# First batch without the limits of later batches, vectors loaded as rows, and an order planned on other durations

## The chip, the cores and the metric

The kernel runs on one core of a Trainium2 chip. The metric is the device time of one execution in microseconds (us); the time of a kernel is the median of its runs. The engines are PE (TensorE matmul, with its weight loads shown as PEld), DVE (VectorE), ACT (ScalarE), POOL (GpSimd) and SP (SyncE, which here only issues DMAs; ACT issues DMAs too).

## What is computed

Sixteen graphs (the batch) of 1024 nodes with 256 features each pass through two layers, all in float32, with a 0/1 adjacency matrix of 1024x1024 per graph. Cut to what matters:

```
# layer 0: attention with 8 heads of 32, masked by adjacency
q, k, v = heads(x @ Wq), heads(x @ Wk), heads(x @ Wv)
e    = leaky(q @ k.T)                      # leaky: max(e, 0.2 e)
attn = softmax(where(adj > 0, e, -9e15), axis=-1)
h    = layernorm(attn @ v) * g1 + b1
x    = layernorm(concat(h, x) @ Wffn.T) * g2 + b2 + x
# layer 1: two graph attentions, then a feed-forward
for W, a in ((W1, a1), (W2, a2)):
    Wh = h @ W
    e  = leaky(Wh @ a[:256] + (Wh @ a[256:]).T)
    h  = softmax(where(adj > 0, e, -9e15), axis=1) @ Wh
h = layernorm(x + h) * g_ln1 + b_ln1
out = layernorm(h + relu(h @ w_ff1 + b_ff1) @ w_ff2 + b_ff2) * g_ln2 + b_ln2
```

The kernel leaves out the shift by the maximum in the softmaxes and counts, per batch, that all sums and scores stay in a safe range. A second, general path follows behind a test of that count; it does not run on these inputs.

## The kernel before, in words

**Work of one batch.** `project` loads x in four pairs of row tiles (`x_pair`, L430, DMA issued by ACT) and transposes them on PE. `mask_part` (L382) loads one tile of 128 rows of the adjacency, as int32 halves of 128x512 (DMA issued by ACT), turns it to 0/-1 in fp8 on DVE (L400), transposes it on PE (L409) and copies it to the mask (ACT, L413). Batch 0 does this in 16 parts of one half each, the other batches in 8 parts of two halves. `qk_part` (L446) projects a group of four heads to q or k for 512 nodes (PE, L460), splits the result in a high and a low half (ACT L463, DVE L465) and stores both to DRAM (SP, L469). `load_stacks` (L521) loads the halves of one head back as stacked operands (SP, L543).

For each of the 8 heads and each of the 8 tiles of 128 keys, one tile of 128x1024 scores goes through a fixed chain: PE multiplies (L576) into a PSUM buffer of which there are two; ACT, or in batch 0 ACT or DVE, scales by 0.2 (L594, L592); DVE takes the maximum with the PSUM tile (L596), which frees the PSUM buffer; ACT takes the exponential (L599); POOL multiplies by the mask (L603); PE sums the weighted values (L625). There are five SBUF buffers `p` for tiles between L594 and L625. That is 64 tiles per batch. `all_scores` takes both PSUM buffers before it issues two tiles of scores; `all_values` consumes two tiles at a time.

The rest of the batch (`rest`, L966: layer norms, the graph attentions L812 to L820, L849 and L874, the feed-forward L914 to L942) runs beside the scores of the following batches.

**What sets the order.** The instruction order of each engine is written out by the program itself. Each piece of work is a generator that yields a cost per engine (`on(PE=..., DVE=...)`), takes and gives buffers of pools, waits for events, and has an aim, a due time. The class `Order` always issues, of the pieces that could start within a window of 300 ns, the one with the earliest aim. The costs and the aims (`AIM`, as shares of `SLOT`, 253 us) decide the order alone: they add no wait. A piece that gets its operands late still waits on the chip, and so does all that stands behind it on its engine. `pace(b)` is the aimed spacing of score pairs: `SLOT/32`, shortened by `fast0`, `fast1` and `fast15` for batches 0, 1 and 15.

**Limits that the planner keeps.** `adj` (2) limits adjacency parts under way, `stage` (2) limits parts of q and k under way, `pair` (18) is the pool of 128x512 float32 buffers for most small tiles. `prepare` (L1010) loads the vectors and weights of the later stages once, beside batch 0; eight vectors are loaded as columns, one number per partition (`load_cols`, L286).

Of the kernel before, what the change touches and what calls it, by code (L numbers as in the profile page):

```python
# [9 lines left out]
FT = mybir.dt.float32  # L10
# [24 lines left out]
class Order:  # L35
# [98 lines left out]
    def run(self):  # L134
        while self.active:
# [33 lines left out]
            if delay:  # L169
                self.transfers = max(self.transfers, end + 1000) + 1450 * max(1, round(cost / 500))  # L170
                th["ready"] = max(end + delay, self.transfers + 1200)
                th["last"] = None, 0
# [52 lines left out]
def unshifted_path(  # L225
# [23 lines left out]
    NSCORE = 4 * NT  # L249
    SLOT = 253e3  # L250
    PACE = SLOT / (H * NT // 2)


    AIM = dict(x=0.818, x_step=0, mask=0.747, mask_step=0.0264, qk0=0.614, qk1=0.898, qk_step=0.0231, v0=0.832,
               v1=0.974, v_step=0.0591, rows=-0.244, rows_step=0.0408, first0=0.12, first1=0.252,
               graph0=-0.009, graph1=0.21, graph_step=0, second=0.355, second_step=0.0335, normed=0.78,
               normed_step=0.026, ff_wait=(None, 0, 1, 0), ff=(0.532, -0.011, 0.487, 0.497), ff_step=0.0386,
               fast0=0.521, fast1=0.85, fast15=0.832, lead=3.15)

# [25 lines left out]

    def load_cols(v, name):  # L286
        t = const.tile([P, v.shape[0] // P], FT, name=name)
        nc.sync.dma_start(t, v.rearrange("(c p) -> p c", p=P), allow_slow_non_contiguous=True)
        return t

    def load_row(v, name):
# [8 lines left out]
    w12 = const.tile([P, DC, YW + 2], FT, name="w12")  # L300
    right = const.tile([P, B, 4], FT, name="right")
    k = {}

# [10 lines left out]
    def evacuate_by(n):  # L314

        return on(DVE=190 + 1.06 * n, ACT=250 + 0.87 * n)

# [65 lines left out]
    def mask_part(b, t, halves):  # L383

        n = len(halves)
        ints = []
        yield take("adj")
        for kh in halves:
# [9 lines left out]
        for i, ai in enumerate(ints):  # L398
# [3 lines left out]
            yield give("pair")  # L402
        yield give("adj")
        yield take("misc")
# [14 lines left out]
    def make_mask(b, t0):  # L419
        yield take("mask")  # L420
        masks[b] = buf([P, NT * N], "mask", "mask", F8)
        parts = [(t, (kh,)) for kh in range(NH) for t in range(NT)] if b == 0 else [(t, (0, 1)) for t in range(NT)]
        for n, (t, halves) in enumerate(parts):
            yield start(mask_part(b, t, halves), t0 + (AIM["mask"] + AIM["mask_step"] * n) * SLOT)

# [20 lines left out]
    def qk_part(b, g, o, nh):  # L446
# [3 lines left out]
        for u in range(nh * 2, nh * 2 + 2):  # L450
            yield wait(("xT", b, u))
        yield take("stage")
        yield take("pair")
# [3 lines left out]
        high, low = (buf([P, HALF], "pair", n) for n in ("high", "low"))  # L457
        yield on(PE=1720)
        for dc in range(DC):
# [11 lines left out]
        yield give("pair")  # L471
        yield give("stage")
        yield fire(("qk", b, g, o, nh))
# [37 lines left out]
    def project(b, t0):  # L511
        yield take("xT")
        xTs[b] = buf([P, DC, N], "xT", "xT")
        for u in range(NP):
            yield start(x_pair(b, u), t0 + (AIM["x"] + AIM["x_step"] * u) * SLOT)
        yield start(make_mask(b, t0), t0 + 0.5 * SLOT)
        for g in range(H // G):
            yield start(project_qk(b, g, t0 + AIM[("qk0", "qk1")[g]] * SLOT), t0)
            yield start(project_v(b, g, t0 + AIM[("v0", "v1")[g]] * SLOT), t0 + (0.8, 1.0)[g] * SLOT)

# [35 lines left out]
    def all_scores():  # L556
        for b in range(B):
            yield wait(("stack", b, 0))
            t0 = begin[b] = work.now
            if b + 1 < B:  # L560
                yield start(project(b + 1, t0), t0)
            for h in range(H):
                yield wait(("stack", b, h))
                q, kk = stacks[b, h]
                for d in range(NT // 2):
                    due = t0 + (h * NT // 2 + d) * pace(b)
                    yield aim(due, AIM["lead"] * PACE)
                    yield take("scores")
                    yield take("scores")
                    ps = [psum.tile([P, N], FT, tag="scores", name="ps_s") for _ in range(2)]  # L570
                    yield on(PE=900)
                    for i in range(2):
                        t = 2 * d + i
                        for nh in range(NH):
                            cols = slice(nh * HALF, (nh + 1) * HALF)
                            nc.tensor.matmul(ps[i][:, cols], kk[:, t * P:(t + 1) * P], q[:, cols],  # L576
                                             start=True, stop=True)
                    if d == NT // 2 - 1:
                        yield give("stacks")
                    for i in range(2):  # L580
                        yield start(weights(b, h, 2 * d + i, ps[i]), due + i * PACE / 2)

# [117 lines left out]
    def rows_pair(b, u):  # L700
# [23 lines left out]
        for i, t in enumerate(tiles):  # L724
            yield on(PE=1720)
            for dc in range(DC):
# [76 lines left out]
    def attend(b, s, big, rows, j, second, sums):  # L803
# [5 lines left out]
        for nh in range(NH):  # L809
            yield wait(("first", b, s, nh))  # L810
        yield on(DVE=1270, shared=True)
        nc.vector.scalar_tensor_tensor(e, first[:, 0, :], second[:, j:j + 1], first[:, 1, :],  # L812
                                       op0=OP.mult, op1=OP.max)
        yield on(DVE=1250, shared=True)
        nc.vector.scalar_tensor_tensor(e, mask_of(b, j), -1.0, e, op0=OP.mult, op1=OP.mult,  # L815
# [29 lines left out]
    def products(pa, cols, big, rows, i, width):  # L845
        for half in range(2):
            yield on(PE=6.68 * width)
            for j in range(half * NT // 2, (half + 1) * NT // 2):
# [14 lines left out]
    def normed_pair(b, u, big, y2):  # L863
# [6 lines left out]
        for i, t in enumerate(tiles):  # L870
            for half in range(2):
                yield on(PE=1720)
                for j in range(half * NT // 2, (half + 1) * NT // 2):
                    nc.tensor.matmul(pa[:, i * D:(i + 1) * D], big[:, j, t * P:(t + 1) * P], y2[:, j, :D],  # L874
                                     start=(j == 0), stop=False)
            yield on(PE=430)
            as_rows(pa, i, x1, i)
# [27 lines left out]
    def hidden(hid, rT, hp, done):  # L905
# [3 lines left out]
        part = hid[hp] = buf([P, 2, 2 * P], "pair", "hid")  # L909
        yield on(PE=1720)  # L910
        for i in range(2):
# [16 lines left out]
    def feed_forward(b, u, rT):  # L928
# [9 lines left out]
        for i in range(2):  # L938
            for half in range(2):
                yield on(PE=1720)  # L940
                for hc in range(half * HC // 2, (half + 1) * HC // 2):
                    nc.tensor.matmul(pa[:, i * D:(i + 1) * D], hid[hc // 2][:, hc % 2, i * P:(i + 1) * P], wf2[:, hc, :],  # L942
                                     start=(hc == 0), stop=False)
            yield on(PE=430)
            as_rows(pa, i, rT, i)
# [64 lines left out]
    def prepare():  # L1010
# [6 lines left out]

        for name, v in (("g1c", g1), ("b1c", b1), ("g2c", g2), ("b2c", b2), ("gl1c", g_ln1), ("bl1c", b_ln1),
                        ("bf1", b_ff1), ("bf2c", b_ff2)):
            yield load(1, 6000)  # L1020
            k[name] = load_cols(v, name)
        for name, v in (("gl2", g_ln2), ("bl2", b_ln2)):
# [26 lines left out]
        def product(wT, dc, by, width):  # L1049
# [4 lines left out]
            return emit  # L1054

        for ic in range(2 * DC):
            yield from piece(300, D, wffnT[:, ic, :], flips(wf, ic))
# [350 lines left out]
```

## Time and profile before

| What | us |
|---|---|
| median of 3 runs | 4526.02 (4524.72 to 4531.43) |
| the profiled execution's own time | 4521.66 |
| its span, first to last instruction | 4519.9 |
| PE busy in the span | 4333.5 |
| DVE busy | 3305.8 |
| ACT busy | 2893.4 |
| POOL busy | 2454.4 |
| first score matmul (L576) of batches 0, 1, 2, 3 starts at | 45.1, 253.8, 510.3, 790.8 |
| of batches 4, 5, ..., 15 at | 1061.4, 1332.1, ..., 4037.8 |
| last matmul of values (L625) of batch 15 starts at | 4297.4 |

How to read it: the span is 1.8 us shorter than the time of the same execution, and the median of the runs is 4.4 us above that execution. The starts of the batches cut the span in stages. From batch 3 on they stand 270.6 us apart, each time. The records of PE in the trace show a float32 matmul as two records and a transpose or a matmul of the stacked scores as one.

### The profile page before, as it was taken

The page shows a single profiled execution, that of the slowest core. Times are in us where ns is not written, and L with a number is a line of the kernel's source. Part 1 is how long each engine was busy: PE and PEld are TensorE (multiplying, and loading weights), DVE is VectorE, ACT ScalarE, POOL GpSimd, SP SyncE. Part 2 cuts the span into 40 slices and gives each one's busy share as a digit, 9 for nine tenths or more (in the row PEclk, how much of TensorE's full clock was granted, in tenths as well). Part 3 has the DMA queues.
Part 4 walks back from the last instruction along what each step waited for, and adds up shares of the span by engine and source line. Part 5 has one row for each costly group of instructions (what it writes and reads, how often), then busy time and mean ns, then how long its engine had stood idle before and what let it go on. Part 6 is the DMA issues. An engine that isn't in the chain of part 4 may idle for free.

```text
span 4519.9 us, 57125 instructions
## 1 busy us (share of the span) xinstructions
PE 4333.5 (96%) x20298; PEld 2875.2 (64%) x20298; DVE 3305.8 (73%) x5246; ACT 2893.4 (64%) x4030; POOL 2454.4 (54%) x1544
## 2 busy tenths in 40 slices
PE   6778999999999999999999999999999999999999
PEld 3345656667666676666667666676666767666587
DVE  4776778777787777768777787777768777776854
ACT  4556666676666666666666666666676676666631
POOL 3655665565565545655565565545655565565710
PEclk8899999999999999999999999999999999999999
DMA  6312323132232322323232232322323232231100
GB/s 177 103 49 73 89 61 109 55 88 76 59 98 64 105 60 74 91 59 110 59 86 73 59 101 68 103 64 70 90 64 102 63 88 67 62 99 49 33 22 20
DMA packets 159109, 343.57 MB, mean 76 GB/s; under 512 B 24673, under 2 KB 27233, under 8 KB 158817
## 3 DMA queue, kind: packets, MB, share of 16 engines
q1 hardware_dynamic: 112736, 255.93, 20.2%
q10 hardware_dynamic: 46080, 83.91, 6.3%
q8 instruction: 164, 2.69, 0.3%
q14 instruction: 129, 1.05, 0.1%
HBM read 239.09 MB, written 100.66 MB: 75 GB/s over the span
## 4 chain that ended last, share of the span: by engine, by line
PE 69%; DVE 17%; POOL 5%; issue 5%; ACT 3%; DMA 0%; ACTq 0%; POOLq 0%; DVEq 0%
PE ps_a L625 15%; PE ps_s L576 9%; PE ps_m L874 7%; PE ps_m L849 7%; PE ps_m L914 7%; PE ps_m L942 6%; POOL p L603 5%; DVE att L812 5%; DVE att L815 5%; DVE p L596 3%; PE ps_m L759 3%; PE ps_m L460 2%; PE ps_m L727 2%; PE ps_m L730 2%; PE ps_m L351 2%
## 5 line engine op out<-in xcount | busy, mean ns | idle before, releaser
L603 POOL TENSOR_TENSOR p<-p,mask 128x1024 f32<-128x1024 f32 x1024 | 2211.6, 2176 | 1645.2 <-ACT p L599 1521.5
L596 DVE TENSOR_TENSOR p<-p,ps_s 128x1024 f32<-128x1024 f32 x1024 | 1210.6, 1214 | 398.1 <-ACT p L594 397.3
L599 ACT ACTIVATE p<-p 128x1024 f32<-128x1024 f32 x1024 | 1081.0, 1058 | 411.6 <-DVE p L596 384.5
L594 ACT ACTIVATE p<-ps_s 128x1024 f32<-128x1024 f32 x993 | 973.6, 1025 | 183.0 <-PE ps_s L576 165.8
L625 PE MATMUL ps_a<-p,v 128*33 128x512 f32 (+1 forms) x4096 | 1005.4, 608 | 49.0 <-POOL p L603 47.6
L576 PE MATMUL ps_s<-qs,ks 128*128 128x512 f32 x2048 | 631.2, 428 | 37.1 <-DVE p L596 35.3
L576 PEld LDWEIGHTS ps_s<-qs,ks 128*128 128x128 f32 x2048 | 352.3, 191 | 338.4 <-DVE p L596 100.0
L625 PEld LDWEIGHTS ps_a<-p,v 128*33 128x33 f32 (+1 forms) x4096 | 198.1, 114 | 560.6 <-issue 398.1
L874 PE MATMUL ps_m<-y,att 128*128 128x256 f32 x2048 | 481.8, 381 | 16.3 <-ACT v L497 13.6
L942 PE MATMUL ps_m<-wf,hid 128*128 128x256 f32 x2048 | 474.0, 381 | 9.4 <-ACT xT L309 8.7
L914 PE MATMUL ps_m<-rT,wf 128*128 128x256 f32 x2048 | 474.7, 381 | 4.0 <-ACT z L309 4.0
L849 PE MATMUL ps_m<-y,att 128*128 128x258 f32 x2048 | 473.3, 381 | 2.8 <-DVE hn L658 2.8
L942 PEld LDWEIGHTS ps_m<-wf,hid 128*128 128x128 f32 x2048 | 379.3, 190 | 78.7 <-issue 15.7
L849 PEld LDWEIGHTS ps_m<-y,att 128*128 128x128 f32 x2048 | 386.4, 190 | 66.8 <-issue 6.0
L874 PEld LDWEIGHTS ps_m<-y,att 128*128 128x128 f32 x2048 | 376.3, 190 | 81.5 <-ACT v L497 16.3
L812 DVE SCALAR_TENSOR_TENSOR att<-first,second 128x1024 f32<-128x1024 f32 x256 | 352.8, 1378 | 81.9 <-ACT first L799 81.9
L914 PEld LDWEIGHTS ps_m<-rT,wf 128*128 128x128 f32 x2048 | 378.4, 190 | 52.9 <-ACT z L309 4.3
L815 DVE SCALAR_TENSOR_TENSOR att<-mask,att 128x1024 f32<-128x1024 fp8e4 x256 | 329.9, 1289 | 8.7
L820 ACT ACTIVATE y<-y,check 128x258 f32<-128x258 f32 x256 | 130.8, 511 | 303.4 <-DVE check L818 283.6
L334 POOL TENSOR_SCALAR rs<-mv 128x2 f32<-128x2 f32 (+1 forms) x224 | 58.8, 262 | 392.5 <-DVE mv L331 392.4
L400 DVE TENSOR_SCALAR adj_b<-adj_i 128x512 fp8e4<-128x512 int32 x256 | 249.4, 1019 | 15.5 <-DMA adj_i<-in_adj_dram 15.5
L923 ACT ACTIVATE hid<-ps_m,bf 128x256 f32<-128x256 f32 x383 | 163.5, 471 | 128.6 <-PE ps_m L914 101.0
(100 smaller groups left out, 4254.7 us busy)
## 6 DMA issues: line engine op xcount, KB each, us to landing
adj_i<-in_adj_dram ACTq DMA_DIRECT2D x256, 256.0 KB, 3.4
qs<-qk_halves SPq DMA_DIRECT2D x256, 256.0 KB, 4.1
ks<-qk_halves SPq DMA_DIRECT2D x256, 256.0 KB, 5.1
qk_halves<-high SPq DMA_DIRECT2D x128, 256.0 KB, 3.2
qk_halves<-low SPq DMA_DIRECT2D x128, 256.0 KB, 3.6
xr<-in_x_dram ACTq DMA_DIRECT2D x64, 256.0 KB, 2.8
x_kept<-x SPq DMA_DIRECT2D x64, 256.0 KB, 2.0
x<-x_kept SPq DMA_DIRECT2D x64, 256.0 KB, 5.4
```

What stands on the lines that cost most here:

```text
L576: nc.tensor.matmul(ps[i][:, cols], kk[:, t * P:(t + 1) * P], q[:, cols], start=True, stop=True)
L594: nc.scalar.activation(p, ps, AF.Copy, scale=ALPHA)
L596: nc.vector.tensor_tensor(p, p, ps, op=OP.max)
L599: nc.scalar.activation(p, p, AF.Exp)
L603: nc.gpsimd.tensor_tensor(p, p, mask_of(b, t), op=OP.mult)
L625: nc.tensor.matmul(acc[nh * 64:nh * 64 + m, :], v[:, t, c:c + m], p[:, nh * HALF:(nh + 1) * HALF], start=(t == 0), stop=(t == NT - 1))
L812: nc.vector.scalar_tensor_tensor(e, first[:, 0, :], second[:, j:j + 1], first[:, 1, :], op0=OP.mult, op1=OP.max)
L815: nc.vector.scalar_tensor_tensor(e, mask_of(b, j), -1.0, e, op0=OP.mult, op1=OP.mult, accum_out=sums[:, j:j + 1])
L849: nc.tensor.matmul(pa[:, cols:cols + width], big[:, j, i * P:(i + 1) * P], rows[:, j, :width], start=(j == 0), stop=(j == NT - 1))
L874: nc.tensor.matmul(pa[:, i * D:(i + 1) * D], big[:, j, t * P:(t + 1) * P], y2[:, j, :D], start=(j == 0), stop=False)
L914: nc.tensor.matmul(pa[:, i * 2 * P:(i + 1) * 2 * P], wf1[:, dc, hc * P:(hc + 1) * P], rT[:, dc, :], start=(dc == 0), stop=(dc == DC - 1))
L942: nc.tensor.matmul(pa[:, i * D:(i + 1) * D], hid[hc // 2][:, hc % 2, i * P:(i + 1) * P], wf2[:, hc, :], start=(hc == 0), stop=False)
```

## The change

It does six things.

1. In batch 0 the adjacency parts no longer take from the pool `adj`. A part of the second half of the columns waits for the same tile's first half instead. So the loads of the adjacency are limited by free buffers of `pair` alone.
2. In batch 0 the parts of q and k no longer take from `stage`.
3. In batch 0 scores are issued one tile at a time, with one PSUM buffer taken, not two tiles with both. Later batches still issue two.
4. x and adjacency of batch 0 are due at once; the adjacency of batch 0 has its own aim, `mask0`.
5. The eight vectors are loaded as rows of 128 numbers (22 rows in all) into the set-up area, transposed by one PE instruction to a tile `columns` of 128x22, and read from there. `load_cols` is gone from this path.
6. Planned costs of several pieces, the planned time of a DMA (800 for 1450), `SLOT` (256 for 253 us) and all aims are other numbers. This gives another order of instructions in all batches.

The diff, cut to its core:

```diff
-                self.transfers = max(self.transfers, end + 1000) + 1450 * max(1, round(cost / 500))
+                self.transfers = max(self.transfers, end + 1000) + 800 * max(1, round(cost / 500))
...
-    SLOT = 253e3
+    SLOT = 256e3
...
-    AIM = dict(x=0.818, x_step=0, mask=0.747, mask_step=0.0264, qk0=0.614, qk1=0.898, qk_step=0.0231, v0=0.832,
-               v1=0.974, v_step=0.0591, rows=-0.244, rows_step=0.0408, first0=0.12, first1=0.252,
-               graph0=-0.009, graph1=0.21, graph_step=0, second=0.355, second_step=0.0335, normed=0.78,
-               normed_step=0.026, ff_wait=(None, 0, 1, 0), ff=(0.532, -0.011, 0.487, 0.497), ff_step=0.0386,
-               fast0=0.521, fast1=0.85, fast15=0.832, lead=3.15)
+    AIM = dict(mask0=0.583, x=0.716, x_step=0.0004, mask=0.525, mask_step=0.0003, qk0=0.528, qk1=0.884,
+               qk_step=0.0266, v0=0.7, v1=1.084, v_step=0.0408, rows=-0.105, rows_step=0.0472, first0=0.106,
+               first1=0.113, graph0=-0.083, graph1=-0.187, graph_step=0.01, second=0.31, second_step=0.0277,
+               normed=0.94, normed_step=0.06, ff_wait=(None, 0, 1, 0), ff=(0.522, 0.127, 0.798, 0.461),
+               ff_step=0.0649, fast0=0.4, fast1=0.492, fast15=0.823, lead=6.1)
...
+    columns = const.tile([P, 32], FT, name="columns")
...
-        return on(DVE=190 + 1.06 * n, ACT=250 + 0.87 * n)
+        return on(DVE=265 + 1.06 * n, ACT=340 + 0.87 * n)
...
-        yield take("adj")
+        if b:
+            yield take("adj")
+        elif halves[0]:
+            yield wait(("mask", b, t, 0))
...
-            yield start(mask_part(b, t, halves), t0 + (AIM["mask"] + AIM["mask_step"] * n) * SLOT)
+            yield start(mask_part(b, t, halves), t0 + (AIM["mask" if b else "mask0"] + AIM["mask_step"] * n) * SLOT)
...
-        yield take("stage")
+        if b:
+            yield take("stage")
...
-            yield start(x_pair(b, u), t0 + (AIM["x"] + AIM["x_step"] * u) * SLOT)
-        yield start(make_mask(b, t0), t0 + 0.5 * SLOT)
+            yield start(x_pair(b, u), t0 + (AIM["x"] + AIM["x_step"] * u if b else 0.0) * SLOT)
+        yield start(make_mask(b, t0), t0 + (0.5 if b else 0.0) * SLOT)
...
-                    yield take("scores")
-                    yield take("scores")
-                    ps = [psum.tile([P, N], FT, tag="scores", name="ps_s") for _ in range(2)]
-                    yield on(PE=900)
-                    for i in range(2):
-                        t = 2 * d + i
+                    for _ in range(n):
+                        yield take("scores")
+                    ps = [psum.tile([P, N], FT, tag="scores", name="ps_s") for _ in range(n)]
+                    yield on(PE=465 * n)
+                    for i in range(n):
...
-        yield on(DVE=1270, shared=True)
+        yield on(DVE=1310, shared=True)
...
-        yield on(DVE=1250, shared=True)
+        yield on(DVE=1330, shared=True)
...
-            yield on(PE=6.68 * width)
+            yield on(PE=6.8 * width)
...
-            yield on(PE=430)
+            yield on(PE=290)
...
-            yield load(1, 6000)
-            k[name] = load_cols(v, name)
+            n = v.shape[0] // P
+            yield load()
+            nc.sync.dma_start(setup[at:at + n, 2620:2620 + P], v.rearrange("(c p) -> c p", p=P))
+            k[name] = columns[:, at:at + n]
+            at += n
...
+        yield from piece(200, lines, columns[:, :lines],
+                         lambda pt: nc.tensor.transpose(pt[:, :lines], setup[:lines, 2620:2620 + P],
+                                                        ident[:lines, :lines]))
```

In `all_scores`, `n` is 2, and 1 for batch 0.

## The prediction

> **What bounds the kernel now.** I first read the page's busy shares and its strip of 40 slices (113 us each).
>
> ```profile
> PE 4333.5 (96%) x20298; PEld 2875.2 (64%) x20298; DVE 3305.8 (73%) x5246; ACT 2893.4 (64%) x4030; POOL 2454.4 (54%) x1544
> ...
> PE   6778999999999999999999999999999999999999
> ...
> PEclk8899999999999999999999999999999999999999
> ```
>
> PE is the bound, except in the first four slices: there it is 60 to 80% busy, and its granted clock is low as well. So I cut the span where the batches' first scores start and asked for the busy time in each stage (columns: stretch, length, then busy us of PE, PEld, DVE, ACT, POOL, the PE clock, the DMA share, GB/s).
>
> ```profile
> 4.00:45.10 41.10, 27.59 (x134) 17.66 (x135) 10.80 (x23) 13.64 (x29) 0.00 (x0) 0.98 0.72 222
> 45.10:253.80 208.70, 159.40 (x598) 65.36 (x599) 146.03 (x147) 115.47 (x139) 132.67 (x64) 0.85 0.41 113
> 253.80:510.30 256.50, 216.82 (x965) 130.05 (x965) 181.67 (x277) 165.79 (x216) 146.07 (x86) 0.95 0.26 71
> 510.30:790.80 280.50, 271.02 (x1272) 178.06 (x1272) 210.26 (x324) 189.13 (x267) 160.69 (x97) 0.99 0.29 84
> 790.80:1061.40 270.60, 266.96 (x1266) 178.38 (x1264) 204.20 (x325) 182.31 (x253) 152.38 (x97) 1.00 0.28 79
> 4297.40:4520.00 222.60, 210.82 (x1032) 182.17 (x1028) 112.56 (x286) 53.41 (x119) 22.20 (x40) 0.99 0.06 21
> ```
>
> From 790.8 on a batch takes 270.6 us, and PE lacks 3.6 us of being full. The tail after the last values is PE work too (210.8 of 222.6). In batch 0's stage no engine is full: PE 76%, DVE 70%, POOL 64%, ACT 55%. That stage is limited by engines waiting for each other. The waits of DVE and of PE in that stretch say how:
>
> ```profile
> DVE p L592 <- PE ps_s L576: 41.0, 24, 5.4
> DVE p L596 <- ACT p L594: 11.5, 4, 6.1
> ```
>
> ```profile
> PE ps_a L625 <- POOL p L603: 26.6, 27, 3.0
> PE ps_s L576 <- DVE p L596: 7.8, 9, 2.5
> ```
>
> DVE waits for a fresh score tile, PE for POOL's masked tile, and behind that wait stand the next scores. It is a loop with too few tiles in flight.
>
> **What the Trainium skill says.** *SBUF — State Buffer*, section "SBUF: two separate sides": DVE and GpSimd share a port pair as an exclusive lock, held for the whole instruction; the loser blocks fully. The trace agrees:
>
> ```profile
> L400 DVE TENSOR_SCALAR adj_b<-adj_i x21: 412/420/2371, 50.6 to 183.5; 128x512 fp8e4<-128x512 int32 x21
> ```
>
> Alone a conversion takes 0.42 us; met by a POOL multiply it takes up to 2.37, and the 21 of this stage average 1.246 us. *TensorE: Matmul & The Clock Gate*, "What's actually happening": the array's clock is gated, and activity releases it. The stages agree (0.85, 0.95, 0.99, 1.00 as PE fills), so a denser start also buys clock. *DMA: Bandwidth & Descriptors*, "Specifications": line rate needs at least 512 B per transfer. The column loads move single numbers and land in 2.4 to 7.6 us for 1 to 4 KB; a 256 KB load of x lands in 2.8 (median). It agrees.
>
> **The yardstick.** I priced PE's instruction order, before and after, with start-to-start times of steady batches: pair of score tiles 1.00 us, group of values (8 records) 1.84, float32 matmul with 512 columns 0.86 (two records of 0.43), with 256 to 260 columns 0.43 to 0.44, with 128 columns 0.23, transposes 0.11 (mask 0.057). A steady batch comes to 262.1 us, so 8.5 of 270.6 is waiting and switching. Summed PE work ahead of the first score of batches 0, 1, 2, 3, 15, and in all:
>
> - before: 24, 143, 343, 606, 3752; 4199
> - after: 22, 142, 336, 596, 3739; 4199
>
> Total work is unchanged (one 22-row transpose more). What can change is the part that is not work, before: 45.1 - 24 = 21 up to batch 0, 208.7 - 119 = 90 in batch 0, 256.5 - 200 = 56 in batch 1, 280.5 - 263 = 17 in batch 2; then 12 x 8.5 = 102, and 482.1 - 447.6 = 34 from batch 15's start to the end. Together 320, and 4199 + 320 is the span.
>
> **Part by part.**
>
> *Loads, adjacency and halves of batch 0.* After, x goes first and eight adjacency halves follow at once on ACT's queue; the stack of head 0 is fetched behind four stores of q and k on SP, before behind six. But all 16 mask parts (11 before) now stand ahead of the first score on PE. Until then x 1.05, weights 0.77, adjacency 4.2, stored halves 4.2 and one stack 1.05 MB must move, 11.3 MB; the first stage moved 222 GB/s at 0.72 share, so 37 us at the 308 that a full share would give, 51 at the same rate. I take 42 us for the first score (3 gained; bounds 37 to 51). ACT issues 12 DMAs ahead of its first copy: the first issues took 0.45 each, a run of four 4.5; its first copy started at 10.0 anyway, so I cost this at nothing, and 0 to 3 us if that cover is gone.
>
> *Single tiles in batch 0.* In PE's order up to 4 tiles were issued beyond the values consumed, falling to 2; after, 6, then 5 falling to 3. A tile's score no longer waits for both PSUM buffers. Floor: POOL, 64 x 2.16 = 138 us, plus about 7 to fill the chain and 5 for conversions that hold its port: 150. From above: DVE was busy 146; 5 conversions fewer x 1.246 leaves about 139. Its 63 us of idle were 41 for scores (1.7 each); with a tile's score due about 0.7 us after its buffer is freed (0.5 matmul and two handovers), 32 x 0.7 = 22, and the other 22 stay: 183. I take 168, nearly midway. PE has 120 us of work in it. Gain 41 (26 to 59).
>
> *Batch 1.* PE work 194. With the waste of batch 2 (17) it would be 211, with its own of before (56) 250. The spacing aimed at is shorter (fast1 0.492 for 0.85), scores get priority, and the first pairs stand only 2.8 to 8 us of PE work apart, less than the chain of a pair takes (about 8), so waits remain. I take 229. Gain 27 (6 to 45).
>
> *Batch 2.* Work 260, waste 13 (8.5 to 17): 273. Gain 7.
>
> *Batches 3 to 14.* Work falls by 3 us in all. Switches between kinds of work on PE: 199 per batch against 194, at 8.5/194 us each 0.2 us. Score pairs and values keep their distances (median 10.2 us of PE work from a tile's score to its values, 10.3 before; shortest 8.2 against 8.6). Unchanged costs by count, so 12 x 270.6 - 3 = 3244. A bound of -2.5 to +2.5 us a batch, from the 3.6 us that PE idles now, gives 30 either way.
>
> *Tail.* The 13 us of work deferred from the start come here: 482 + 13 = 495. It is PE work that fills PE; unknown handovers ±5.
>
> *Vectors as rows.* Eight loads stay eight issues on SP (median about 0.48 us). The transpose and one copy add 0.11 and about 0.2 us, and they stand ahead of the other set-up pieces. First use is in batch 1, some 100 us later, so nothing; without that cover the slower landing, 4 us, would be the most at stake.
>
> Sum: 42 + 168 + 229 + 273 + 3244 + 495 = 4451, against a span of 4519.9: 69 less, 1.5%. The profiled execution took 4521.66 and the median of runs is 4526.0, so 4457 for the median.
>
> **Rivals.**
>
> - *The loop stays tight.* DVE and POOL still block each other (16 conversions now fall among POOL's multiplies, some in fours, which took 5.3 us of DVE each time before), and ACT's and DVE's in-order side work delays each tile. Batch 0 takes 190, batch 1 250, batch 2 280: 42 + 190 + 250 + 280 + 3244 + 495 = 4501, median 4507. For it: no engine is full now. Against: tiles in flight do rise.
> - *Steady batches get worse.* All adjacency parts of a batch are now aimed at one time (mask_step 0.0003 for 0.0264) and the feed-forwards elsewhere. If DVE blocks in bursts, scores come late and PE idles, 13 times over. The gain of 69 is gone from 5.3 us a batch (PE's idle 3.6 becoming 9); at 10 us a batch the time is 4457 + 130 = 4587, slower than before. Against: in DVE's order the conversions of a steady batch still stand mostly in pairs among the maxima, as before.
> - *Steady batches get better too.* Better prices could take 2 us from each: 4457 - 26 = 4431; with the start at its floor (150, 211) it would be near 4395.
> - *Nothing.* The starts gain and the deferred work comes back as waits in the tail: 4526.
>
> **Chances and range.** The forecast, 4425 to 4490 by its own bounds, 66%; tight loop 13%; better everywhere 8%; nothing 4%; worse steady batches 9%. A difference under about 0.2% (9 us) can't be told from no change here. Faster 0.87, same 0.04, slower 0.09. The range 4405 to 4510 leaves out the slower case, the null and the ends of the others.
>
> **What would show it.** First scores of batches 0 to 3 near 42, 210, 439 and 712; in batch 0 the wait of L592's successor for scores near 20 us, POOL at 80% or more, a clock of about 0.9; then starts 270 us apart. It is wrong if batch 0 stays above 190 us, or if the steady distance moves by more than 3 us.

## The result: 9 us faster, where 69 were forecast

| | time, us (median, lowest to highest) | ratio to before |
|---|---|---|
| before | 4526.51 (4524.0 to 4531.43, 19 runs) | 1 |
| after | 4517.23 (4512.8 to 4523.15, 19 runs) | 0.998 [0.9973, 0.9988] |

The changed kernel is faster by 0.2%; that is small, but the whole interval lies below 1. The profiled execution took 4516.56 us, with a span of 4514.8. The page of the changed kernel, the same lines as of before:

```profile
PE 4340.4 (96%) x20299; PEld 2887.7 (64%) x20299; DVE 3332.3 (74%) x5272; ACT 2891.4 (64%) x4005; POOL 2480.1 (55%) x1544
...
PE   7988999999999999999999999999999999999999
...
PEclk9999999999999999999999999999999999999999
```

The first slices are fuller, the clock higher, and one thing has grown: DVE is busy 26.5 us more. It has 26 instructions more and ACT 25 fewer: copies that the planner gave to the other engine, some 19 us by their own durations. Behind the rest stand larger shifts at equal counts: DVE's conversions of the adjacency (L399) take 86 us less over the whole run, its attention steps (L814, L817) 54 us more. Where the time went shows when the span is cut at the first scores of batches 0, 1, 2, 3 and 5, and at the last values (columns as before: stretch, length, busy us of PE, PEld, DVE, ACT, POOL, clock, DMA share, GB/s):

```profile
41.10:199.00 157.90, 137.65 (x583) 58.75 (x582) 145.18 (x141) 114.20 (x141) 133.85 (x65) 0.96 0.48 132
199.00:455.80 256.80, 217.49 (x949) 128.04 (x947) 184.78 (x267) 166.12 (x215) 153.72 (x85) 0.93 0.29 82
455.80:738.80 283.00, 269.13 (x1268) 176.84 (x1266) 227.30 (x332) 181.11 (x250) 167.53 (x98) 0.99 0.28 80
738.80:1022.80 284.00, 266.79 (x1253) 176.98 (x1251) 226.04 (x324) 179.12 (x251) 165.69 (x95) 0.99 0.26 75
1295.00:1567.60 272.60, 268.40 (x1266) 179.83 (x1264) 202.01 (x327) 182.78 (x253) 152.22 (x97) 0.99 0.28 78
4293.00:4514.80 221.80, 211.33 (x1040) 183.96 (x1036) 117.29 (x297) 49.54 (x108) 20.65 (x40) 0.99 0.06 21
```

Batch 0 fell from 208.7 to 157.9 us, 51 where 41 were forecast for it. Batch 1 did not follow (256.8, 256.5 before), batches 2 and 3 are longer (283.0 and 284.0 for 280.5 and 270.6), and a steady batch takes 1.7 us more. In batches 2 and 3 DVE is busy 226 to 227 us where before's batch 3 needed 204.20.

In batch 0 the waits of DVE (first fence) and of PE (second) moved as the step on single tiles said; L594 and L598 are before's L592 and L596:

```profile
DVE p L594 <- PE ps_s L578: 7.4, 12, 1.4
```

```profile
PE ps_s L578 <- DVE p L598: 14.2, 18, 2.8
...
PE ps_a L627 <- POOL p L605: 3.2, 6, 1.0
```

DVE's wait for scores fell from 41.0 to 7.4 us, PE's for POOL from 26.6 to 3.2; what is left is PE's wait for the maxima (14.2, before 7.8). POOL is busy 85% of the stage. DVE's conversions still meet POOL's multiplications at times (the longest takes 2.38 us), but no long wait of PE ends on them; in the first 200 us (least, median, longest in ns):

```profile
L399 DVE TENSOR_SCALAR adj_b<-adj_i x32: 412/427/2377, 9.3 to 139.9; 128x512 fp8e4<-128x512 int32 x32
```

The terms of the prediction beside what the trace measured (first score to first score):

| Term | forecast | measured | difference |
|---|---|---|---|
| first score | 42 | 41.1 | -0.9 |
| batch 0 | 168 | 157.9 | -10.1 |
| batch 1 | 229 | 256.8 | +27.8 |
| batch 2 | 273 | 283.0 | +10.0 |
| batch 3 | 270.3 | 283.9 | +13.6 |
| batches 4 to 14 | 2973.7 | 2994.9 | +21.2 |
| tail | 495 | 497.0 | +2.0 |

The differences sum to 64 us. So there are two questions: what holds batches 1 to 3 (51 us), and what costs a steady batch 2 us more than forecast, 1.7 more than before (21 us in all).

### The profile page after: what moved, and what is told of

It is laid out like the page before. It is cut to its first block, busy times and chain, and to the rows that moved or that the text cites. A ratio compares the mean times of both kernels' runs of the same rounds, so it can differ in the third digit from the quotient of the medians.

```text
span 4514.8 us, 57089 instructions
## 1 busy us (share of the span) xinstructions
PE 4340.4 (96%) x20299; PEld 2887.7 (64%) x20299; DVE 3332.3 (74%) x5272; ACT 2891.4 (64%) x4005; POOL 2480.1 (55%) x1544
## 3 DMA queue, kind: packets, MB, share of 16 engines
q14 instruction: 128, 1.05, 0.1%
## 4 chain that ended last, share of the span: by engine, by line
PE 67%; DVE 24%; ACT 3%; issue 2%; DMA 1%; POOL 1%; ACTq 0%; SPq 0%; DVEq 0%; POOLq 0%
PE ps_a L627 15%; PE ps_m L851 9%; PE ps_s L578 9%; PE ps_m L876 8%; DVE p L598 6%; PE ps_m L916 6%; PE ps_m L944 6%; DVE att L817 5%; DVE att L814 4%; PE ps_m L761 3%; PE ps_m L729 2%; PE ps_m L732 2%; PE ps_m L347 2%; DVE z L957 2%; PE ps_m L461 2%
## 5 line engine op out<-in xcount | busy, mean ns | idle before, releaser
L605 POOL TENSOR_TENSOR p<-p,mask 128x1024 f32<-128x1024 f32 x1024 | 2244.6, 2207 | 1373.7 <-ACT p L601 1266.3
L598 DVE TENSOR_TENSOR p<-p,ps_s 128x1024 f32<-128x1024 f32 x1024 | 1216.2, 1214 | 449.5 <-ACT p L596 447.4
L596 ACT ACTIVATE p<-ps_s 128x1024 f32<-128x1024 f32 x992 | 975.3, 1022 | 200.6 <-PE ps_s L578 188.4
L627 PE MATMUL ps_a<-p,v 128*33 128x512 f32 (+1 forms) x4096 | 990.1, 603 | 14.2 <-POOL p L605 13.8
L627 PEld LDWEIGHTS ps_a<-p,v 128*33 128x33 f32 (+1 forms) x4096 | 200.3, 113 | 497.8 <-issue 399.6
L876 PE MATMUL ps_m<-y,att 128*128 128x256 f32 x2048 | 483.8, 382 | 17.1 <-DVE hn L660 14.6
L851 PE MATMUL ps_m<-y,att 128*128 128x258 f32 x2048 | 494.8, 390 | 4.4 <-ACT hid L925 2.0
L851 PEld LDWEIGHTS ps_m<-y,att 128*128 128x128 f32 x2048 | 392.9, 195 | 88.3 <-issue 20.4
L814 DVE SCALAR_TENSOR_TENSOR att<-first,second 128x1024 f32<-128x1024 f32 x256 | 364.8, 1425 | 40.1 <-ACT first L801 40.1
L817 DVE SCALAR_TENSOR_TENSOR att<-mask,att 128x1024 f32<-128x1024 fp8e4 x256 | 371.8, 1453 | 8.7
L925 ACT ACTIVATE hid<-ps_m,columns 128x256 f32<-128x256 f32 x374 | 160.5, 471 | 103.7 <-PE ps_m L916 88.6
L341 DVE TENSOR_SCALAR y<-y,mv,rs 128x256 f32<-128x256 f32 x256 | 181.3, 749 | 25.5 <-POOL rs L332 24.0
```

Source lines behind the costliest of these rows:

```text
L596: nc.scalar.activation(p, ps, AF.Copy, scale=ALPHA)
L598: nc.vector.tensor_tensor(p, p, ps, op=OP.max)
L605: nc.gpsimd.tensor_tensor(p, p, mask_of(b, t), op=OP.mult)
L627: nc.tensor.matmul(acc[nh * 64:nh * 64 + m, :], v[:, t, c:c + m], p[:, nh * HALF:(nh + 1) * HALF], start=(t == 0), stop=(t == NT - 1))
L851: nc.tensor.matmul(pa[:, cols:cols + width], big[:, j, i * P:(i + 1) * P], rows[:, j, :width], start=(j == 0), stop=(j == NT - 1))
```

## The experiments

All stage lengths below are from the traces, first score to first score; "4 to 14" is the mean of the eleven batches. Each ratio is to runs of before on the same chip as that run.

| Run | time | ratio to before | first score | b0 | b1 | b2 | b3 | 4 to 14 | tail |
|---|---|---|---|---|---|---|---|---|---|
| before | 4526.5 | 1 | 45.1 | 208.7 | 256.5 | 280.5 | 270.6 | 270.6 | 482.1 |
| after | 4517.2 | 0.998 | 41.1 | 157.9 | 256.8 | 283.0 | 283.9 | 272.3 | 497.0 |
| e1 | 4539.4 | 1.0031 [1.0018, 1.0044] | 46.4 | 182.0 | 267.6 | 299.4 | 277.9 | 270.8 | 485.7 |
| e2 | 4572.9 | 1.0106 [1.0089, 1.0123] | 37.8 | 201.8 | 250.5 | 299.2 | 287.4 | 272.8 | 496.6 |
| e3 | 4555.8 | 1.0077 [1.006, 1.0094] | 39.8 | 159.8 | 258.4 | 302.8 | 304.8 | 271.8 | 496.8 |
| e4 | 4544.4 | 1.0043 [1.0026, 1.0059] | 41.1 | 157.9 | 259.8 | 286.9 | 286.1 | 274.1 | 497.8 |
| e5 | 4491.2 | 0.9919 [0.9905, 0.9932] | 47.5 | 170.3 | 256.3 | 283.7 | 270.6 | 270.7 | 483.9 |
| e6 | 4463.9 | 0.9864 [0.9849, 0.9879] | 41.3 | 159.2 | 227.9 | 268.7 | 269.9 | 272.1 | 497.0 |
| e7 | 4470.2 | 0.9874 [0.9859, 0.9889] | 40.5 | 159.8 | 257.8 | 282.6 | 285.7 | 268.1 | 494.2 |
| e8 | 4520.0 | 0.9987 [0.998, 0.9993] | 41.3 | 158.1 | 259.9 | 283.0 | 284.0 | 272.4 | 495.9 |
| e9 | 4506.2 | 0.996 [0.9945, 0.9975] | 45.5 | 183.4 | 258.3 | 281.3 | 270.6 | 270.5 | 488.8 |
| e10 | 4502.9 | 0.9947 [0.9932, 0.9963] | 46.0 | 184.7 | 256.5 | 285.4 | 270.6 | 270.6 | 483.1 |
| e11 | 4478.7 | 0.9895 [0.988, 0.991] | 40.0 | 159.2 | 257.9 | 284.1 | 287.4 | 268.9 | 489.5 |
| e12 | 4491.9 | 0.9926 [0.9913, 0.994] | 46.0 | 173.0 | 253.7 | 281.5 | 270.6 | 270.6 | 485.7 |
| e13 | 4521.3 | 0.9988 [0.9981, 0.9994] | 45.9 | 170.5 | 256.3 | 281.6 | 274.1 | 273.0 | 486.3 |
| e14 | 4550.8 | 1.0053 [1.0037, 1.007] | 42.0 | 157.9 | 263.6 | 299.0 | 297.2 | 272.2 | 495.6 |

### e1 and e2: the first-batch edits and the plan, each alone

e1 is the kernel before with edits 1 to 4; e2 is the changed kernel with the limits of batch 0 put back.

```diff
-        yield take("adj")
+        if b:
+            yield take("adj")
+        elif halves[0]:
+            yield wait(("mask", b, t, 0))
...
-        yield take("stage")
+        if b:
+            yield take("stage")
...
+                n = 2 if b else 1
```

> Edits 1 to 4 alone (no limits in batch 0, single tiles, things due at once) on the plan of before (its aims, costs and SLOT; vectors as columns). Theory A, order pays later: the start gains as in the changed kernel (batch 0 from 209 to about 160 us), and the later batches cost what their own order costs; from batch 5 on the order is that of before, so 270.6 us a batch; batches 1 and 2 have graph attentions mixed with maxima and cost as much as before or 5 us more. Time about 4485 (4475 to 4497). Theory B, a gain at the start is always taken back by later waits, whatever the plan: about 4517, like the changed kernel.

> The new plan (aims, costs, SLOT, rows) with the limits of batch 0 put back (adjacency and q/k limits, two tiles of scores at once). Theory A: batch 0 takes 200 to 210 us again, and from batch 4 on the order is that of the changed kernel, 272.3 us a batch against 270.6: slower than before, about 4540 (4530 to 4560). Theory B: the sum hardly depends on the start: about 4517.

Both theories missed e1: batch 0 gained only 27, and batches 1 to 3 lost 37, although the steady batches came out as before. The time of e2 lies above both theories; its batch 0 of 201.8 is theory A's, so the edits, and not the new plan alone, made batch 0 short. Batches 2 and 3 of e2 are longer than in either kernel, and the steady ones take 272.8. So the 1.7 us by which a steady batch is longer belong to the new plan, and the loss in batches 2 and 3 comes with more than one order: e1, e2 and the changed kernel each have another one there, and all three show it.

### e3 and e4: moving DVE's work inside the order

In the new order the attention steps (L814, L817, sixteen of each per batch) stand between the maxima of batches 2 and 3; before's batch 3 has them in two blocks of eight. (In before only the first eight of batch 2, which takes 280.5 us, are mixed; in the changed kernel the first eight of batch 1 and all sixteen of batches 2 and 3.) Two lines of each kernel, by groups, batch 3 alone (columns: operation and tile, count, then busy us and mean ns of one, then idle before). Before:

```profile
L812 DVE SCALAR_TENSOR_TENSOR att<-first,second 128x1024 f32<-128x1024 f32 x16 | 21.6, 1352 | 5.6 <-ACT first L799 5.6
L815 DVE SCALAR_TENSOR_TENSOR att<-mask,att 128x1024 f32<-128x1024 fp8e4 x16 | 19.6, 1225 | 0.5
```

After:

```profile
L817 DVE SCALAR_TENSOR_TENSOR att<-mask,att 128x1024 f32<-128x1024 fp8e4 x16 | 37.7, 2359 | 0.6
L814 DVE SCALAR_TENSOR_TENSOR att<-first,second 128x1024 f32<-128x1024 f32 x16 | 27.7, 1733 | 2.7 <-ACT first L801 2.7
```

L817 takes 1.23 us in a block and 2.36 on average between maxima: in this batch ten took about 3.04 us and six 1.22. All long ones overlap one of POOL's multiplications; of the whole run's 256, the 218 that met none took 1.22 to 1.23. It fits the exclusive lock that the Trainium skill describes in *SBUF — State Buffer*, "SBUF: two separate sides": a DVE operation with two inputs in SBUF, as these have, and a GpSimd operation that reads SBUF can't use the shared port pair together; the one that comes second waits until the other is done. The records agree, and the wait is part of the busy time they show.

Together the two lines take 24 us more a batch, which covers DVE's growth of 21.8 between the two batches. e3 puts the steps of batches 0 to 2 in blocks, at the place of the eighth:

```diff
+        held = holds.setdefault((b, s), ([], []))
+        if b < 3:
+            held[0].append(att)
+            if len(held[0]) == NT:
+                for emit in held[0] + held[1]:
+                    emit()
```

> The changed kernel with the same order on PE and POOL, but in the rest of batches 0 to 2 the eight graph attention steps of DVE (L814, L817) stand in one block, where the last of them stood, not mixed with the maxima (ACT's row scalings move with them). Theory A, the mixed steps meet POOL's multiplies at the shared port: the steps fall from 1.73 and 2.36 us to about 1.35 and 1.23 in batch 3, and batch 3 falls from 284 to about 272, batch 2 from 283 to about 275; time about 4497 (4490 to 4506). Theory C, batches 2 and 3 are long for the order of PE and not for this: their lengths stay within 3 us, time 4512 to 4522.

The steps did become cheap (DVE 206.42 us of batch 2's 302.80), and yet batches 2 and 3 grew by 20 each, and the time lies above both theories. PE now waits in a few long stretches, here over those two batches:

```profile
PE ps_m L893 <- ACT hid L942: 17.7, 1, 17.7
PE ps_m L868 <- DVE low L466: 16.5, 1, 16.5
PE ps_s L578 <- DVE p L598: 16.4, 3, 13.7
```

Theory A falls as it was put: cheap steps are not enough. A block of 21 us holds up every maximum behind it. The edit moved ACT's row scalings behind the block too, so how much of the 20 us is DVE's alone is not shown.

e4 turns to the steady batches. Of batches 5 to 14 of the changed kernel eight have one window of 3.4 us at half clock, some 124 us after their start, and take 272.5 to 272.8; the two without it take 270.9 and 271.0. Ahead of it L955 and L957, the two last operations of the last layer norm, stand in front of a maximum and take up to 2.35 us in place of 0.48 where they meet POOL. In batch 5 (start, length, then what; in brackets the wait ahead of it):

```profile
1414.08 2.35 DVE L955 SCALAR_TENSOR_TENSOR z<-z,mv,gl 128x256 f32<-128x256 f32 x1
1416.46 0.48 DVE L957 SCALAR_TENSOR_TENSOR z<-z,rs,bl 128x256 f32<-128x256 f32 x1
1416.86 2.35 DVE L598 TENSOR_TENSOR p<-p,ps_s 128x1024 f32<-128x1024 f32 x2
...
1418.13 0.73 PE L578 MATMUL ps_s<-qs,ks 128*128 128x512 f32 x2 [1.49 <-DVE p L598]
```

e4 puts them two maxima later:

```diff
+        if b + 3 < B:
+            late.append([2, emit, ("out", b, u)])
+            yield wait(("out", b, u))
```

> The changed kernel with the same order on PE, POOL and ACT, but for batches 0 to 12 the last layer norm's four steps on DVE (L955, L957) stand two maxima later, and the store behind them too. Theory A, those steps delay the maxima, PE idles 1.9 us within one clock window, and the next window runs at half clock: the half-clock window at 124 us of each steady batch is gone, a steady batch takes about 270.7 us for 272.3, time about 4502 (4495 to 4508). Theory C, the steady batches are longer for other waits: 272 us, half-clock windows remain or move, 4512 to 4522.

The window at 124 us went, as theory A said, but others came at 229 us (275.4 to 275.9 in such batches), and the batches without one took 272.7. That is theory C in kind, though the time (4544.4) lies above its range too. The one other place tried is worse.

### e5: the new batch 0 in front of before's order

e5 is e1 with one aim, `fast0`, at 0.44. From about 53 us into batch 1 to the end, the order of every engine in the trace is then that of before; the expectation says from batch 1's start, which is not quite so.

```diff
-               fast0=0.521, fast1=0.85, fast15=0.832, lead=3.15)
+               fast0=0.440, fast1=0.850, fast15=0.832, lead=3.15)
```

> Edits 1 to 4 of the change on the plan of before (vectors, costs, aims of before), with the one aim fast0 at 0.44, in place of 0.521. In this plan the order of every engine from the start of batch 1 to the end is that of before, instruction for instruction; only batch 0 and what stands ahead of it differ. Theory A (batch 0's gain is real, and it was the other order of the later batches that gave it back): the first score at 46 and batch 0 in 160 to 175 us, then the batches of before (256.5, 280.5, 270.6, ...) and its tail of 482, so some 41 less than before: 4485 (4478 to 4497). Theory C (a faster first batch is given back later whatever the order, since the later batches wait for something that batch 0 doesn't make faster): batches 1 to 3 grow by 20 or more together, time 4510 or more.

Theory A: batch 0 took 170.3 and the rest within 7 us of what it took before; the median is 35.8 us less, the span 29.8 (the traced run of before was 4 us under its median). Of the 36 us gained up to batch 1's first score (253.8 to 217.8) the span keeps 30 when the order behind is left alone; of the changed kernel's 54.8 it keeps 5.

### e6 and e7: the changed order with less DVE work

e6 leaves out L814 in batches 0 to 2, e7 leaves out L957 in batches 0 to 12; nothing else moves.

```diff
+        if b > 2:
             nc.vector.scalar_tensor_tensor(e, first[:, 0, :], second[:, j:j + 1], first[:, 1, :],
...
+            if b > 12:
                 nc.vector.scalar_tensor_tensor(row, row, rs[:, i:i + 1], k["bl2"], op0=OP.mult, op1=OP.add)
```

> The changed kernel with the first of the two DVE operations of an attention step (L814, the leaky step) left out in the graph attentions of batches 0, 1 and 2; the second (L817) reads the first exponential instead of its result. That leaves out part of the computation: 48 instructions, 76.7 us of DVE, 16 each in batches 1, 2 and 3. The order of all else is the same on every engine. Theory A (batches 1 to 3 are long because DVE's attention steps hold up the maxima and POOL): batch 1 falls from 256.8 to 242 or less, batches 2 and 3 from 283 and 284 to 274 or less; time 4485 or less. Theory C (they are long because of the places of PE's own instructions, which wait for handovers of a fixed length): each falls by less than 4; time 4507 or more.

> The changed kernel with the last operation of the last layer norm (L957, DVE, 8 a batch) left out for batches 0 to 12, which leaves out part of the computation; the order of all else is the same. Theory A (the 1.65 us by which a steady batch with a half-clock window is longer come from L955 and L957 standing ahead of a maximum while POOL holds the port): the windows at 124 us of a batch go, batches 4 to 14 take 271.0 each, time 4503 (4500 to 4507). Theory C (the order has other tight places that take it over): the batches stay within 0.5 of 272.3, time 4512 to 4520.

e6 is theory A: batches 1, 2 and 3 took 227.9, 268.7 and 269.9, where the prediction had 229, 273 and 270.3. The windows of e6, batches 1 to 3:

```profile
200.50:428.40 227.90, 208.33 (x948) 123.77 (x946) 157.54 (x251) 164.54 (x215) 150.41 (x85) 0.99 0.32 92
428.40:697.10 268.70, 265.30 (x1268) 176.26 (x1267) 188.44 (x316) 180.19 (x250) 160.20 (x98) 1.00 0.30 84
697.10:967.00 269.90, 262.85 (x1252) 176.76 (x1250) 190.79 (x308) 178.73 (x250) 155.43 (x95) 1.00 0.27 78
```

In batches 2 and 3 the same PE order runs at full clock and as tight as a steady batch as soon as DVE has 76.7 us less to do in the three batches (and L817 becomes shorter too, 1.61 us on average for 2.21). So PE's order and its handovers alone were not what held them. The mechanism shows in the changed kernel's batch 1, in stretches of 10 us; there the second attention of batch 0 stands in one block on DVE:

```profile
379.00:389.00 10.00, 9.96 (x57) 5.89 (x54) 5.25 (x8) 7.04 (x13) 5.36 (x3) 1.00 0.56 164
389.00:399.00 10.00, 3.47 (x15) 1.78 (x14) 9.76 (x15) 3.29 (x7) 0.00 (x0) 0.98 0.01 2
399.00:409.00 10.00, 0.74 (x2) 0.66 (x3) 9.72 (x18) 2.04 (x4) 0.00 (x0) 0.50 0.00 0
```

DVE is full for 20 us; POOL does nothing, PE almost nothing, and its clock halves. By the trace PE waits for a small division of the head's output (L660), which frees a PSUM buffer and stands behind the block on DVE. A maximum (L598) comes directly after it:

```profile
PE ps_m L876 <- DVE hn L660: 14.6, 1, 14.6
...
407.78 0.42 DVE L660 TENSOR_TENSOR hn<-ps_m,check 128x256 f32<-128x256 f32 x1
408.12 1.21 DVE L598 TENSOR_TENSOR p<-p,ps_s 128x1024 f32<-128x1024 f32 x1
```

The division itself takes 0.42 us. It is the block of 21 us in front of it that costs PE 14.6; moving the division alone ahead of the block would by this order have freed little, since the next pair of scores needs the buffer that this maximum frees at 409.3 us. Leaving out L814 shortens the block, and the same wait is 4.3 us in e6.

In e7 the direction is theory A's, and the size was too small: the batches took 268.0, not 271.0. The half-clock windows went (each is worth 1.65 us in its batch), and so did the wait ahead of them and some more. In ten batches of the changed kernel this was PE's largest wait, which e7 does not show at all:

```profile
PE ps_s L578 <- DVE p L598: 18.8, 20, 1.5
```

So one operation, busy 10.7 us in such a batch (107.1 in ten), holds 4 us of it.

### e8: the vectors alone

```diff
-            nc.sync.dma_start(setup[at:at + n, 2620:2620 + P], v.rearrange("(c p) -> c p", p=P))
+            nc.sync.dma_start(columns[:, at:at + n], v.rearrange("(c p) -> p c", p=P), allow_slow_non_contiguous=True)
```

> The changed kernel with the eight vectors loaded as columns again, straight to the tile they are read from; the transposing piece is kept, on other data, so that the order of all engines is that of the changed kernel. Theory A (the vectors are loaded beside batch 0 and first read some 100 us later, so the way they are loaded costs nothing): within 0.2% of the changed kernel, 4517 (4509 to 4526). Rival (the column loads, of one number per partition, hold up the loads behind them on their queues or the stores of q and k): 4526 or more, with batch 0 above 160.

Theory A: the same as the changed kernel but for batch 1, which took 259.9 us. In e4, which has the changed kernel's order and its row loads up to there, it took 259.8, so the 3 us are no sign of the columns. They cost nothing that shows here, and so rows gain nothing.

### e9 and e10: which edit shortened batch 0

Both have `fast0` at 0.44 and, in batches 1 to 14, before's order; in batch 15 and the tail the order differs somewhat. e9 is the kernel before with single tiles alone; e10 is e5 with pairs again, so it has the edits of the loads alone:

```diff
-                n = 2 if b else 1
+                n = 2
```

> The kernel before with edit 3 alone (single score tiles in batch 0) and fast0 at 0.44; from batch 1 on the order of every engine is that of before. Theory A (the two PSUM buffers taken together are what limits batch 0; the prediction put all of batch 0's gain to this edit): batch 0 from 208.7 to 180 or less, time 4498 or less. Theory B (the loads of adjacency, x, q and k hold batch 0 as well, so single tiles without edits 1, 2 and 4 bring less than half): batch 0 at 190 or more, time 4508 or more.

> The kernel before with edits 1, 2 and 4 (no limits on loads in batch 0, x and adjacency due at once), score tiles in pairs as before, and fast0 at 0.44; from batch 1 on the order of every engine is that of before. Theory A (the pairs limit batch 0): batch 0 at 198 or more, time 4516 or more. Theory B (the loads do): 185 or less, time 4503 or less.

Batch 0: 208.7 before, 183.4 with single tiles, 184.7 with the loads' edits, 170.3 with both (e5), 157.9 in the changed kernel. e9 lies between its two theories, e10 meets B. With `fast0` at 0.44, each alone brings 24 or 25, both 38. That aim has a part in it: with both edits and `fast0` at 0.521, which is e1, batch 0 took 182.0, so 12 of the 38 came with the aim. Its part in e9 and e10 was not measured.

### e11: L957 on POOL, with everything computed

```diff
-            nc.vector.scalar_tensor_tensor(row, row, rs[:, i:i + 1], k["bl2"], op0=OP.mult, op1=OP.add)
+                nc.gpsimd.tensor_scalar(row, row, rs[:, i:i + 1], None, op0=OP.mult)
+                nc.gpsimd.tensor_tensor(row, row, k["bl2"], op=OP.add)
```

> The changed kernel with the last operation of the last layer norm (L957, one of DVE) done by POOL in batches 0 to 12, as two operations of 128x256 (scale by a column, add a row), at the same place of the order; everything is computed. Leaving it out gave batches of 268.0 and 4470. Theory A (what counts is that DVE's maxima come earlier, and POOL, busy 153 of 272 us, has room): batches of 268 to 270, time 4470 to 4492. Theory C (POOL does its instructions in order, so its multiplications come later by what the 16 operations take, and they hold the port against DVE): batches of 272 or more, time 4513 or more.

Theory A: steady batches of 268.8, and 4478.7 us, the fastest kernel of this study that computes everything, 1.05% below before. POOL pays for it, ten steady batches:

```profile
L960 POOL TENSOR_SCALAR z<-z,rs 128x256 f32<-128x256 f32 x80 | 81.8, 1022 | 49.7 <-DVE z L955 32.4 <-issue 11.7 <-POOL rs L332 5.5
L961 POOL TENSOR_TENSOR z<-z,bl 128x256 f32<-128x256 f32 x80 | 58.4, 730 | 6.7
```

That is 14 us of POOL a batch in place of 10.7 of DVE, and still a gain of 3.4: POOL had the room, and in this order PE's longest waits ended on DVE (18.8 of its 41.5 us of waits in ten batches on the maxima, 12.0 and 3.4 on other work of DVE).

### e12 and e13: can the gains be added

e12 is e5 with the changed kernel's aims for batch 0's x, adjacency, q, k and v, but `mask0` at 0.52 and `fast0` at 0.43; e13 is e5 with e11's edit.

> As the run in which all later orders were those of before (4491), but with the projections, x and adjacency of batch 0 on the aims of the changed kernel and fast0 at 0.43; batches 3 to 14 have the order of before, 1 and 2 nearly. Theory A (batch 0's gain stays when the later order is one that DVE keeps up with): first score at 41 to 47, batch 0 in 158 to 170, the rest within 4 us of before, time 4470 to 4492. Theory C (what is gained ahead of batch 1 beyond 40 us is given back): 4495 or more.

> Both gains together: the first batch of the run with before's later order (4491), and the last operation of the last layer norm (L957 of the changed kernel) on POOL in batches 0 to 12, at the same place. Theory A (a steady batch of before's order is also held by DVE's side work): it falls from 270.6 to 268.8 as in the changed kernel's order, time 4467 to 4476. Theory B (in before's order no PE wait of a steady batch ends on a DVE maximum: its waits end on ACT's copies and on POOL; so DVE's relief brings nothing): batches within 0.5 of 270.6, or longer by what POOL's later multiplications add, time 4486 or more.

The time of e12 is at the edge of theory A, no better than e5: batch 0 took 173.0, above the range given. So these aims are not what takes the changed kernel from 170 to 157.9; what does stays open (`fast0` at 0.4, `lead` and the planned costs differ as well). e13 is theory B, and worse: 273.0 a batch and 4521.3. In before's order no wait of PE in a steady batch ended on DVE; in ten batches its waits ended on ACT's copies (27.6 us) and on POOL (8.1), and POOL's new work made the latter longer:

```profile
PE ps_a L631 <- POOL p L609: 23.8, 30, 1.0
```

That is 16 us of the 23 lost in ten batches. The same edit gains 3.4 us a batch in one order and loses 2.3 in the other.

### e14: DVE's time, or the port

```diff
+        if b < 3:
+            nc.gpsimd.tensor_scalar(e, first[:, 0, :], second[:, j:j + 1], None, op0=OP.mult)
```

> As the run without L814 in batches 0 to 2 (4464), but POOL multiplies by the column in its place, 16 times 128x1024 in each of batches 1, 2 and 3; the maximum of the leaky step is still left out. DVE is relieved as in that run, while POOL works some 30 to 45 us more a batch and holds the port as much longer. Theory A1 (DVE's own time is what made batches 1 to 3 long): within 5 us of that run's 227.9, 268.7 and 269.9, time 4460 to 4475. Theory A2 (the port that DVE and POOL share is what made them long, so the work counts whichever of the two does it): batches 1 to 3 together 25 us or more above that run, time 4490 or more.

Batches 1 to 3 are 93 us above e6, as A2 said and A1 did not. But the run settles neither cause: the groups of batches 1 to 3 show DVE also waiting for POOL's product, which stands in POOL's own queue.

```profile
L815 POOL TENSOR_SCALAR att<-first,second 128x1024 f32<-128x1024 f32 x48 | 161.5, 3368 | 0.0
...
L820 DVE SCALAR_TENSOR_TENSOR att<-mask,att 128x1024 f32<-128x1024 fp8e4 x48 | 132.3, 2757 | 72.6 <-POOL att L815 72.6
```

72.6 us of the loss can be that queue. That the attention work holds batches 1 to 3 is shown (e6); how much of it is DVE's own time and how much the meetings at the port stays open. e6 took both away: an estimate from the durations is 61 us of DVE's own time (48 times L814 at 1.27 alone) and 44 us of meetings (the rest of L814's 76.7, and the 28.7 by which L817 got shorter). Taking POOL's multiplications away to part the two was not tried.

## Why the prediction was wrong

- *Loads and first score* (42): right, 41.1.
- *Single tiles* (168 for batch 0, all of the gain put to this edit): inside the range, 157.9. The upper sum kept 44 us of DVE's idle time where 12.7 were left, and took 7 us off DVE's work where 1 went. The attribution was too simple: with `fast0` at 0.44, single tiles brought 25 of the 51 (e9), the loads' edits 24 (e10) and both 38 (e5); the last 12 are not explained.
- *Batch 1* (229): the failed step. The prediction took PE's work and added a waste between those of other batches, on the ground that PE is the bound. It allowed 35 us for what is not PE's work; 63 were measured, of which 29 go when L814 is left out (227.9 in e6). That this comes within 2 us of 229 is chance: 229 was chosen between 211 and 250, and e6 leaves an operation out. What failed is that batch 1 also carries 16 attention steps, 41 us of DVE at the durations of before's batch 3, and the prediction did not ask what stands behind them on DVE.
- *Batch 2* (273) and *batch 3* (270.3, "unchanged costs by count"): failed by the same step. It allowed 13 and 8 us beside PE's work; 23 and 22 were measured. The counts did stay; the durations did not. Steps mixed with maxima meet POOL and take 24 us more a batch. With L814 out, 268.7 and 269.9.
- *Batches 4 to 14* (-0.25 us each): mechanism missed. The rival that steady batches get worse had the right place, DVE in bursts ahead of scores, but named the conversions; it was mostly the last layer norm (e7, e11), and 1.7 us a batch, not the 5.3 from which it would have decided.
- *Tail* (495): right, 497.0.
- *Vectors* (nothing): right (e8).
- *Signs of being wrong*: neither came. Batch 0 stayed under 190 us and the steady distance moved by 1.7. The first scores of batches 2 and 3, forecast near 439 and 712 and measured at 455.8 and 738.8, were the ones to watch. The rival of a tight loop had batches 1 and 2 near what came (250 and 280), but put that to batch 0's loop, which came out fast.

The gain of the start is therefore real: 54.8 us up to batch 1's first score (253.8 to 199.0). It was spent again in later orders that changed along with it (under before's aims too, as e1 shows): 16 in batches 1 to 3, 19 in batches 4 to 14, 15 in the tail, each against before, which leaves the 5 by which the spans differ. Of the tail's 15 the prediction had 13, as work of PE put off from the start. In e5 the same three parts cost 3, 2 and 2 us.

## What to carry to other kernels

Where the order of every engine is fixed, price each engine's order, not only that of the fullest one: an operation costs what is queued behind it, and here a block of 21 us on DVE cost PE 14.6 us, through a division of 0.42 us queued behind it. An operation moved between engines or by two places can gain or lose according to which wait ends last in that very order, so a gain from one order is no promise for another (e11, e13). Before replanning everything with a local edit, look for the plan that leaves the other orders as they are; here such a plan was 26 us faster than the changed kernel (e5), though its batch 0 is 12 us longer.

## What the hardware showed that was not expected

- POOL takes longer to multiply a 128x1024 tile by a column than by another tile: 2.83 to 3.82 us, with 3.81 in the median (e14), against 2.11 for the quickest multiplications by the mask in the same run and 2.14 in the median. In 128x256 the column took 0.92 at least and adding a row 0.72 (e11).
- DVE's maxima, one input of which is in PSUM, took 1.19 to 1.22 us in all 1024 cases of the changed kernel, also where they overlapped one of POOL's multiplications. L817, with both inputs in SBUF, took 1.22 us clear of them and mostly about 3.04 where it met one. So the lock is narrower than the prediction's words for it: not every operation of DVE is held up.
- PE idled 1.9 us, in two waits of 1.49 and 0.40 close together (1416.6 to 1419.3 us of the changed kernel), and a window of 3.4 us at half clock followed: eight matmul records of L851 took 3.05 us there, where sixteen took 3.65 just before.
